# Two places in PSUM for half sums m1; columns of weights and means in one bank; first means in the images' places; another order in the beginning

## The chip, the cores and the metric

The kernel runs on one core of one Trainium2 chip. The metric is the device time of one execution in microseconds (us). The engines are named as in the profile: PE (matrix multiplication; PEld is its loading of weights), DVE (vector), ACT (scalar), POOL (general) and SP (which issues most transfers). Each engine takes its instructions in the order in which the program wrote them; an instruction that has to wait holds up all that stands behind it on its engine.

## What is computed

The input x has 160 images of 128 channels with 32x32 pixels. Each image is normalised over groups of four channels, then convolved (3x3, 128 to 128 channels, padding 1) with a weight set that is first quantised in two steps; there are five weight sets, each for 32 of the images. The result is added to x.

```python
beta, alpha = jnp.max(U), jnp.min(U)
s1 = (beta - alpha) / 3.0
v1 = s1 * floor(U / s1)
s2 = s1 / 5.0
v2 = s2 * floor((U - v1) / s2)
w = (v1 + v2).reshape(OUT_CH * N, IN_CH, K, K)          # N = 5 sets
act = conv_general_dilated(xb, w, strides (1, 1), padding 1, feature_group_count=N)
...
g = v.reshape(B_, 32, C_ // 32, H_, W_)                 # _gn: groups of 4 channels
m, s = mean(g, axis=(2, 3, 4)), var(g, axis=(2, 3, 4))
normalised = (g - m) / sqrt(s + eps)
x = x + conv(_gn(x), U)
```

## The kernel before

**One image.** The channels lie on the 128 partitions. The normalised image is kept as two float16 parts, a high one and a low one, which are convolved one after the other into the same sums. The 3x3 window is done as three columns of taps, in the order `COLS` = 1, 0, 2. Rows are taken in pairs: an even and an odd row of the output share products with sums and differences of rows of the input. The products with sums of rows are gathered in PSUM tile `m1`, those with differences in tile `m2` (16 half rows x 32, one bank each). An image's own sums stand in a pair of banks, `eo`; two such pairs take turns.

There are two kinds of images from image 7 on: even ones ("parted") take six matmuls for the half sums, 18 direct ones with the high part (line 629) and 12 short ones (line 668); odd ones ("combined") work on sums of rows for both parts and take 12 matmuls for half sums and 24 for the rest, all of line 668. Images 0 to 2 (`FIRST` = 3) are convolved without half sums; image 2 stands in the banks of m1 and m2 meanwhile.

**The order of one step.** `conv(i)` writes for PE: the half sums of the next image, `sums_of_pairs(i + 1)` (line 668: differences into m2, then sums into m1), and then the rest of image i, `rest_of_column`, on top of what `pairs(i)` has put into `eo`. After that ACT copies m2 of image i+1 to SBUF (`leave`, line 725) and DVE writes m1 + m2 and m1 - m2 into the next `eo` (`pairs`, lines 735 and 737). So in one step of the loop PE's sums for image i+1 must not overwrite m1 before DVE's line 737 has read it for image i, and PE's first matmul of the rest of image i needs line 737 as well. Between the two stand three matmuls of sums (parted) or six (combined).

Around this ACT measures later images (lines 194 and 201, sum and square), normalises (523, 531, 576) and takes finished images out of PSUM at half size (`residual`, line 754); POOL adds them to x by a transfer (773) and does the small arithmetic of the statistics (221 to 246) and two outer rows of a combined image (554, 555); DVE makes the low parts (589, 582) and the sums of rows (603 to 606, 565 to 571), measures some images itself (184 to 188) and quantises the next weight set in small portions (101 to 127, 463).

**Statistics of a group of images.** `means` is a matmul (line 210) into a small PSUM tile `pg`; ACT copies it (219, `ngm`); POOL makes deviations `dv` (221 to 224); `variances` is a second matmul (227) into `pg`; ACT reads it (233, `ve`), POOL makes `rstd` and `shift` (237 to 246), which `normalise` needs. **Columns of weights.** `turn_column` transposes three taps into PSUM tile `pt` (line 472); ACT writes them as `wt` (485) and, halved, as `half` (486); POOL makes four more from `half` (487 to 490). `pg` and `pt` have a bank each, m1 and m2 one each, `eo` four: all eight banks.

**The beginning.** Nothing is scheduled by a planner: the order on each engine is the order of the calls in `run`. For the first three images the calls are: the range of all weights (DVE), statistics 0 and 1, the three columns of set 0, direct products of images 0 to 2 column by column, and then the first three rounds of the loop, in which `residual` 2, 0 and 1, `measure(0, 11)` (image 11 is measured on DVE), `leave(3)`, `pairs(3)`, `low_part(4)` and `combinations(4)` stand. `sums_of_pairs(3)` is written in round 2.

Of the kernel before, what the change touches and what calls it, by code (L numbers as in the profile page):

```python
# [19 lines left out]
ROW = 3  # L20
# [139 lines left out]
class Statistics:  # L160
# [2 lines left out]

    size = 1024

    def __init__(self, nc, small, psum, gavg, mhalf, nb, scale, name):
        self.nc, self.small, self.psum, self.gavg, self.mhalf = nc, small, psum, gavg, mhalf
        self.nb, self.scale, self.name = nb, scale, name

        self.mv = self.tile("mv", [nb, 2])  # L170
# [32 lines left out]
            accum_out=self.mv[:, j, 1:2],  # L203
        )

    def means(self):
        self.pg = self.psum.tile(
            [self.nc.NUM_PARTITIONS, 2, self.nb], F32, tag="pg", name=f"pg{self.name}"
        )
        self.nc.tensor.matmul(  # L210
            self.pg[:, 0, :], self.gavg, self.mv[:, :, 0], start=True, stop=True
        )
# [36 lines left out]
def general_path(tc, keep, steps, x, u, out):  # L249
# [8 lines left out]
    with tc.If(far > 0), ExitStack() as ctx:  # L258
        one = ctx.enter_context(tc.tile_pool(name="g_one", bufs=1))
        psum = ctx.enter_context(tc.tile_pool(name="g_psum", bufs=1, space=PSUM))  # L260
        ident = one.tile([P, P], F32, tag="ident", name="g_ident")
        make_identity(nc, ident)
        gavg = group_mean_matrix(nc, one)
        mhalf = one.tile([P, 1], F32, tag="mhalf", name="g_mhalf")
        nc.gpsimd.memset(mhalf, -0.5)
        pad = one.tile([P, H + 2, W + 2], F32, tag="pad", name="g_pad")
        nc.gpsimd.memset(pad, 0.0)
        for n in range(N_SETS):
            un = one.tile([P, C, TAPS], F32, tag="u", name=f"g_u{n}")
            nc.sync.dma_start(un, uv[n])  # L270
            wn = one.tile([P, C, TAPS], F32, tag="w", name=f"g_w{n}")
            k1, k2 = run(steps.quantise(one, un, f"g{n}", F32))
            nc.vector.tensor_scalar_mul(wn, k1, steps.s1)
            nc.vector.scalar_tensor_tensor(wn, k2, steps.s2, wn, ALU.mult, ALU.add)
            wt = one.tile([P, TAPS, C], F32, tag="wt", name=f"g_wt{n}")
            for k in range(TAPS):
                pt = psum.tile([P, C], F32, tag="pt", name=f"g_pt{n}_{k}")
                nc.tensor.transpose(pt, wn[:, :, k], ident)
                nc.scalar.copy(wt[:, k, :], pt)
            with tc.For_i(0, IMGS // N_SETS, 1) as b:  # L280
                xt = one.tile([P, H * W], F32, tag="xt", name=f"g_xt{n}")
                nc.sync.dma_start(xt, xv[n, :, bass.ds(b, 1), :])
                stats = Statistics(nc, one, psum, gavg, mhalf, 1, 1.0, f"g{n}")
                stats.image(0, xt)
                stats.means()
# [24 lines left out]


class Main:
# [36 lines left out]
    def __init__(self, tc, ctx, keep, x, u, out):  # L349
# [9 lines left out]
        def pool(name, bufs, **kw):  # L359
# [15 lines left out]
        self.small = pool("small", 3)  # L375
        self.ps_eo = pool("ps_eo", 2, space=PSUM)
        ps_m = pool("ps_m", 1, space=PSUM)
        self.ps_stat = pool("ps_stat", 1, space=PSUM)
        self.ps_tr = pool("ps_tr", 1, space=PSUM)
        self.steps = Steps(nc, keep)  # L380

        self.pair = [
            ps_m.tile([P, self.H // 2, self.W], F32, tag=name, name=name) for name in ("m1", "m2")
        ]
        self.chunks, self.z, self.hi, self.v, self.eo, self.m2 = {}, {}, {}, {}, {}, {}
        self.sum = {}
        self.wts = {}
# [49 lines left out]
    def over_partitions(self, ext1, ident, between):  # L437


        nc, P = self.nc, self.P  # L440
        rows = self.ps_tr.tile([1, 2, P], F32, tag="pt", name="rows")
# [5 lines left out]
        spread = self.ps_tr.tile([P, 2], F32, tag="pt", name="spread")  # L447
        nc.tensor.matmul(spread, self.ones, top, start=True, stop=True)
        return spread

    def make_column(self, n, col, by_scalar=False):
# [5 lines left out]
        k1, k2 = yield from self.steps.quantise(self.qpool, un, f"{n}_{col}", MM, by_scalar)  # L457
        if n == 0:
            parts = ((k1, self.ident5), (k2, self.ident))
            self.keep_column(n, col, self.turn_column(n, col, parts))  # L460
# [5 lines left out]

    def turn_column(self, n, col, parts):
        nc, P = self.nc, self.P
        pt = self.ps_tr.tile([P, ROW, P], F32, tag="pt", name=f"pt{n}_{col}")
# [6 lines left out]
        return pt  # L476

    def keep_column(self, n, col, pt):


        nc, P = self.nc, self.P
        wt = self.wpool.tile([P, 6, P], MM, tag=f"wt{col}", name=f"wt{n}_{col}")
        half = self.qpool.tile([P, ROW, P], MM, tag="half", name=f"half{n}_{col}")
        outer = self.qpool.tile([P, P], MM, tag="outer", name=f"outer{n}_{col}")
        nc.scalar.mul(wt[:, self.G, :], pt, 2.0 / LIFT)  # L485
        nc.scalar.mul(half, pt, 1.0 / LIFT)
# [4 lines left out]
        self.wts[n, col] = wt  # L491


    def by_vector(self, i):
# [2 lines left out]
    def stats_of(self, k):  # L497
        if k not in self.stats:
            self.stats[k] = Statistics(
                self.nc, self.small, self.ps_stat, self.gavg, self.mhalf, len(self.groups[k]),  # L500
                self.steps.lift, k,
            )
        return self.stats[k]
# [160 lines left out]
    def product(self, target, i, kind, source, col, start, stop):  # L664
# [9 lines left out]
            skip_group_check=True,  # L674
        )

    def both(self, i):

        return [self.halves(v) for v in ([self.hi[i]] if self.combined(i) else []) + [self.v[i]]]

    def sums_of_pairs(self, i):

        both = self.both(i)
        for a, kind in ((1, self.DIFF), (0, self.SUM)):
            for col in self.COLS:
                for j, (_, st) in enumerate(both):
                    self.product(
                        self.pair[a], i, kind, st[:, a], col,
                        col == self.COLS[0] and j == 0,
                        col == self.COLS[-1] and j == len(both) - 1,  # L690
                    )
# [30 lines left out]
    def leave(self, i):  # L722

        m2 = self.evac.tile([self.P, self.H // 2, self.W], F32, tag="m2", name=f"m2_{i}")
        self.nc.scalar.copy(m2, self.pair[1])  # L725
        self.m2[i] = m2

    def pairs(self, i, between=lambda: None):


        nc = self.nc
        m1, m2 = self.pair[0], self.m2.pop(i)
        eo = self.eo[i] = self.bank_pair(i)
        rows = eo.rearrange("p h (i a) w -> p (h i) a w", a=2)
        nc.vector.tensor_add(rows[:, :, 0], m1, m2)  # L735
# [46 lines left out]
    def run(self):  # L782
# [44 lines left out]
        spread = self.over_partitions(ext1, ident, self.stats_of(0).means)  # L827

        def take(steps, count):
            for _ in range(count):  # L830
# [25 lines left out]
        self.stats[0].scales()  # L856
        take(second, 1)
        measure(1, 3)
        self.stats[1].means()
        self.stats[1].deviations()  # L860
        self.warm_up(14)
        parts(0)
# [3 lines left out]
        self.stats[1].scales()  # L866
        parts(1)
        run(first)
        self.warm_up(2)
        parts(2)  # L870
        take(second, 2)
# [11 lines left out]
        take(third, 1)  # L883
        measure(1, 4)
        run(second)
        measure(1, 5)
        parts(3)
        measure(0, 6, 7)
        measure(1, 6, 7)
        for i in range(self.FIRST):  # L890
# [11 lines left out]
        for i in range(self.imgs):  # L902
# [3 lines left out]
            def on_the_way(col):  # L906
                if col == self.COLS[1]:
                    for st in ready:
                        st.means()
                    for *column, parts in self.columns:  # L910
                        turned.append((column, self.turn_column(*column, parts)))
                    self.columns.clear()
                if col == self.COLS[2]:
                    for st in middle:
# [29 lines left out]
            if i < self.FIRST:  # L944
# [5 lines left out]
                if i == 2:  # L950
# [44 lines left out]
            if i < self.FIRST:  # L995
                for st in ready:
                    st.deviations()
            for column, pt in turned:
                self.keep_column(*column, pt)
            turned = []  # L1000

            if i >= self.FIRST:
# [70 lines left out]
```

## Time and profile before

| | |
|---|---|
| median of 4 runs | 992.46 us (991.67 to 993.86) |
| the profiled execution | 992.15 us, of which its span is 990.3 us |
| PE busy | 958.2 us, 97% |
| DVE busy | 927.7 us, 94% |
| ACT busy | 894.6 us, 90% |
| POOL busy | 386.3 us, 39% |
| bytes moved | 246.05 MB, mean 248 GB/s |

The span is the time from the first to the last instruction; 1.8 us of the execution lie around it. PE's clock was granted in full nearly throughout (mean 0.999). In the 40 slices of the page PE is busy 2 tenths in the first, 8 in the second, 9 or more in all others but the last (7). The views used below are the page, the waits (who waited for whom, in total), the chain of waits (followed back from the last instruction), the timeline of an engine (start, length, line, operation, output<-input), and the windows (busy time by stretch). One thing is needed to read PE's lines: matmuls overlap, and their ends are modelled. A matmul of 512 columns is given 379 ns, but the next one starts 216 ns after it when nothing holds it up.

### The profile page before, as it was taken

The numbers are of one execution on the slowest core, as the hardware profiler recorded it, in microseconds if no ns is written. First come the engines' busy times: TensorE is split into PE (matmuls) and PEld (weight loads), VectorE is DVE, ScalarE is ACT, GpSimd is POOL, SyncE is SP. The second block draws the span as 40 slices with busy tenths as digits, with TensorE's granted clock in tenths as the row PEclk, the third lists the DMA queues.
The fourth block names the chain that finished last, engine by engine and source line by source line (L and its number), as shares of the span: only waits on it lengthen the run. The fifth ranks groups of instructions, "written<-read, shape, count | busy, mean of one in ns | idle before, by whom it ended". The sixth has DMA issues, their size and how long they took to land.

```text
span 990.3 us, 16124 instructions
## 1 busy us (share of the span) xinstructions
PE 958.2 (97%) x5938; PEld 578.4 (58%) x5938; DVE 927.7 (94%) x1256; ACT 894.6 (90%) x1224; POOL 386.3 (39%) x565
## 2 busy tenths in 40 slices
PE   2899999999999999999999999999999999999997
PEld 1445655566656666666655666666665666666564
DVE  7999999999999999989999999999999998889995
ACT  5879999999999999999999999999999999998651
POOL 4324563633316253714343433315343424132410
PEclk9999999999999999999999999999999999999999
DMA  9538999999997989799898999998999898987764
GB/s 361 207 107 237 243 252 274 256 264 273 256 310 176 297 238 304 190 301 266 261 252 253 267 278 238 281 284 222 241 277 305 214 301 217 291 227 206 181 177 153
DMA packets 65129, 246.05 MB, mean 248 GB/s; under 512 B 5008, under 2 KB 5008, under 8 KB 65040
## 3 DMA queue, kind: packets, MB, share of 16 engines
q1 hardware_dynamic: 45312, 173.09, 50.0%
q0 software_dynamic: 19728, 71.84, 37.7%
q8 instruction: 48, 0.79, 0.3%
q14 instruction: 41, 0.34, 0.1%
HBM read 89.19 MB, written 83.89 MB: 175 GB/s over the span
## 4 chain that ended last, share of the span: by engine, by line
PE 72%; DVE 12%; ACT 7%; issue 3%; POOL 3%; DMA 2%; SPq 0%; DVEq 0%; ACTq 0%; POOLq 0%
PE eo L668 24%; PE m L668 24%; PE eo L629 23%; ACT junk L201 2%; ACT vh L576 2%; DVE eo L737 1%; DVE eo L735 1%; ACT sum L754 1%; DMA xt<-in_x_dram 1%; DVE lo L589 1%; DVE v L565 1%; POOL v L554 1%; POOL rstd L237 1%; DVE vl L582 1%; ACT m L725 1%
## 5 line engine op out<-in xcount | busy, mean ns | idle before, releaser
L668 PEld LDWEIGHTS <-wt 128*128 128x128 f16 x4266 | 417.2, 98 | 234.9 <-issue 6.5
L629 PE MATMUL eo<-hi,wt 128*128 128x496 f16 (+3 forms) x1422 | 339.6, 375 | 1.4 <-ACT wt L485 0.9
L773 POOL DMA_DIRECT2D xt<-sum x137 | 122.4, 899 | 463.8 <-ACT sum L754 449.6
L629 PEld LDWEIGHTS <-wt 128*128 128x128 f16 x1494 | 146.0, 99 | 141.9 <-ACT wt L485 2.3
L582 DVE SCALAR_TENSOR_TENSOR vl<-v,rstd,vh 128x2048 f16<-128x2048 f32 x80 | 188.1, 2351 | 4.3 <-ACT vh L576 4.3
L668 PE MATMUL eo<-vh,wt 128*128 128x248 f16 (+1 forms) x960 | 183.9, 273 | 0.0
L668 PE MATMUL eo<-vl,wt 128*128 128x248 f16 (+1 forms) x960 | 183.9, 273 | 0.0
L668 PE MATMUL m<-vh,wt 128*128 128x496 f16 (+1 forms) x480 | 182.2, 380 | 1.8 <-DVE eo L737 1.1
L668 PE MATMUL m<-vl,wt 128*128 128x496 f16 (+1 forms) x480 | 182.2, 380 | 0.2 <-DVE vl L582 0.2
L194 ACT ACTIVATE junk<-xt 128x1024 f16<-128x1024 f32 x152 | 160.6, 1057 | 17.5 <-DMA xt<-in_x_dram 13.9
L201 ACT ACTIVATE junk<-xt,mv 128x1024 f16<-128x1024 f32 x152 | 173.8, 1144 | 0.1
L576 ACT ACTIVATE vh<-v,rstd 128x2048 f16<-128x2048 f32 x80 | 160.8, 2011 | 2.5 <-POOL v L555 2.0
L754 ACT ACTIVATE sum<-eo 128x1024 f32<-128x1024 f32 x137 | 138.0, 1008 | 14.9 <-PE eo L668 14.8
L735 DVE TENSOR_TENSOR eo<-m,m 128x512 f32<-128x512 f32 x157 | 109.2, 695 | 36.3 <-ACT m L725 28.4
L668 PE MATMUL eo<-rows,wt 128*128 128x256 f16 (+1 forms) x924 | 138.9, 273 | 0.0
L668 PE MATMUL m<-rows,wt 128*128 128x496 f16 (+1 forms) x462 | 113.6, 380 | 0.5 <-DVE eo L737 0.2
L737 DVE TENSOR_TENSOR eo<-m,m 128x512 f32<-128x512 f32 x157 | 109.5, 697 | 3.6
L725 ACT COPY m<-m 128x512 f32<-128x512 f32 x157 | 90.5, 577 | 18.4 <-PE m L668 18.4
L523 ACT ACTIVATE z<-xt,shift,rstd 128x1024 f32<-128x1024 f32 x80 | 99.8, 1248 | 2.7 <-POOL shift L244 2.6
L589 DVE TENSOR_TENSOR lo<-z,hi 128x1024 f16<-128x1024 f32 x80 | 97.9, 1224 | 0.0
L565 DVE TENSOR_TENSOR v<-xt 128x960 f32<-128x960 f32 x80 | 92.0, 1149 | 0.0
L531 ACT CAST hi<-z 128x1024 f16<-128x1024 f32 x80 | 83.6, 1045 | 2.5
(111 smaller groups left out, 890.5 us busy)
## 6 DMA issues: line engine op xcount, KB each, us to landing
xt<-in_x_dram SPq DMA_DIRECT2D x78, 1024.0 KB, 9.5
out_dram<-xt SPq DMA_DIRECT2D x78, 1024.0 KB, 6.0
xt<-sum POOLq DMA_DIRECT2D x137, 512.0 KB, 6.2
u<-in_L_conv_U_dram SPq DMA_DIRECT2D x4, 576.0 KB, 9.0
xt<-in_x_dram SPq DMA_DIRECT2D x4, 512.0 KB, 9.5
range<-in_L_conv_U_dram SPq DMA_DIRECT2D x3, 576.0 KB, 7.6
out_dram<-xt SPq DMA_DIRECT2D x3, 512.0 KB, 2.8
u<-in_L_conv_U_dram SPq DMA_DIRECT2D x2, 288.0 KB, 2.9
```

Of the source, the lines that this page charges most:

```text
L194: self.nc.scalar.activation(junk, image, ACTF.Copy, scale=-1.0 / image.shape[1], accum_out=self.mv[:, j, 0:1],)
L201: self.nc.scalar.activation(junk, image, ACTF.Square, bias=self.mv[:, j, 0:1], accum_out=self.mv[:, j, 1:2],)
L565: nc.vector.tensor_sub(v[:, W:last], x[:, : last - W], x[:, 2 * W :])
L576: self.nc.scalar.mul(vh, self.v[i], st.rstd[:, j])
L582: self.nc.vector.scalar_tensor_tensor(vl, self.v[i], st.rstd[:, j], self.hi[i], ALU.mult, ALU.subtract)
L589: self.nc.vector.tensor_sub(lo[:, 1 : self.H + 1, :].rearrange("p h w -> p (h w)"), self.z.pop(i), self.hi[i].rearrange("p h w -> p (h w)"),)
L629: nc.tensor.matmul(self.bank(target, h)[:, r0 - h0 : r1 - h0, c0:c1], self.wts[n, col][:, k, :], tile[:, s0 : s0 + r1 - r0, c0 + dw : c1 + ...
L668: self.nc.tensor.matmul(target[:, :, c0:c1], self.wts[n, col][:, kind, :], source[:, :, c0 + dw : c1 + dw], start=start, stop=stop, skip_g ...
L735: nc.vector.tensor_add(rows[:, :, 0], m1, m2)
L737: nc.vector.tensor_sub(rows[:, :, 1], m1, m2)
L754: nc.scalar.mul(self.sum[i], eo.rearrange("p h r w -> p (h r w)"), 0.5)
L773: self.nc.gpsimd.dma_start(self.image(i), self.sum.pop(i), accum_op=ALU.add)
```

## The change

- m1 gets two places, `m1a` for images with even number and `m1b` for odd ones, in banks of their own; m2 stays one. Image 2 stands in m1a and m2.
- Eight banks being all there are, `pt` (384 columns) and `pg` (the other 128) become parts of one tile `small` in one bank. The first two groups' means lie in a pair of banks of `eo` that is not yet in use, and so do the rows for the weight range.
- `keep_column` is cut in three: `keep_taps` (wt), `keep_halves` (half) and `keep_sums` (POOL's four). For column 2 of set 0 the calls are now taps, means of group 2, halves, deviations of group 2, sums.
- `measure(0, 11)` moves from the end of round 1 to round 2, between `pairs(3)` and `low_part(4)`.

In the written order of the instructions PE, ACT and SP keep theirs. On POOL the four instructions of `keep_sums` of that column move behind the four of `deviations`. On DVE the five instructions of image 11's measurement move behind the two of `pairs(3)`. The number of instructions is the same on every engine. Of the waits, the one of the first sum into m1 for line 737 is gone in each step, and the loading of weights for the first matmul of `rest_of_column` waits for line 737 in its place. The matmul of group 2's means now waits for ACT's `wt` of column 2, and ACT's `half` waits for that matmul. At a later set's columns the transposing matmul waits for ACT's last reading of the shared bank.

```diff
-        self.ps_stat = pool("ps_stat", 1, space=PSUM)
-        self.ps_tr = pool("ps_tr", 1, space=PSUM)
+        ps_small = pool("ps_small", 1, space=PSUM)
...
-        self.pair = [
-            ps_m.tile([P, self.H // 2, self.W], F32, tag=name, name=name) for name in ("m1", "m2")
-        ]
+        self.m1a, self.m1b, self.m2_ps = (
+            ps_m.tile([P, self.H // 2, self.W], F32, tag=name, name=name)
+            for name in ("m1a", "m1b", "m2")
+        )
+        self.pair = [self.m1a, self.m2_ps]
+
+        small = ps_small.tile([P, 512], F32, tag="small", name="small")
+        self.pt, self.pg = small[:, : ROW * P].rearrange("p (k o) -> p k o", k=ROW), small[:, ROW * P :]
...
+    def m1(self, i):
+        return self.m1b if i % 2 else self.m1a
...
                     self.product(
-                        self.pair[a], i, kind, st[:, a], col,
+                        self.m2_ps if a else self.m1(i), i, kind, st[:, a], col,
...
-        m1, m2 = self.pair[0], self.m2.pop(i)
+        m1, m2 = self.m1(i), self.m2.pop(i)
...
-        self.stats[2].means()
+
+        self.keep_taps(0, self.COLS[2])
+        self.stats[2].means(self.pg)
+        half = self.keep_halves(0, self.COLS[2])
         self.stats[2].deviations()
+        self.keep_sums(0, self.COLS[2], half)
...
                     self.high_part(5)
                     self.pairs(3)
+                    measure(0, 11)
                     self.low_part(4)
                     run(self.combinations(4))
                 self.residual(j)
-                if i == 1:
-                    measure(0, 11)
```

More of the change, by code (lines that the diff above doesn't have):

```diff
@@ L164, with __init__ @@
     size = 1024
-    def __init__(self, nc, small, psum, gavg, mhalf, nb, scale, name):
-        self.nc, self.small, self.psum, self.gavg, self.mhalf = nc, small, psum, gavg, mhalf
+    def __init__(self, nc, small, gavg, mhalf, nb, scale, name):
+        self.nc, self.small, self.gavg, self.mhalf = nc, small, gavg, mhalf
         self.nb, self.scale, self.name = nb, scale, name
@@ L204, in image_square, with means @@
         )
[L206 to L209, printed above, removed]
+    def means(self, place):
+        self.pg = place[:, : 2 * self.nb].rearrange("p (k j) -> p k j", k=2)
         self.nc.tensor.matmul(
@@ L282, in general_path @@
                 nc.sync.dma_start(xt, xv[n, :, bass.ds(b, 1), :])
-                stats = Statistics(nc, one, psum, gavg, mhalf, 1, 1.0, f"g{n}")
+                stats = Statistics(nc, one, gavg, mhalf, 1, 1.0, f"g{n}")
                 stats.image(0, xt)
-                stats.means()
+                stats.means(psum.tile([P, 2], F32, tag="pg", name=f"g_pg{n}"))
                 stats.deviations()
@@ L440, in over_partitions @@
         nc, P = self.nc, self.P
-        rows = self.ps_tr.tile([1, 2, P], F32, tag="pt", name="rows")
+        place = self.bank_pair("range").rearrange("p h r w -> p h (r w)")
+        rows = place[0:1, 0, : 2 * P].rearrange("p (k c) -> p k c", k=2)
         for k in range(2):
@@ L446, in over_partitions @@
         nc.vector.tensor_reduce(top, rows, AX.X, ALU.max)
-        spread = self.ps_tr.tile([P, 2], F32, tag="pt", name="spread")
+        spread = place[:, 1, :2]
         nc.tensor.matmul(spread, self.ones, top, start=True, stop=True)
@@ L459, in make_column @@
             parts = ((k1, self.ident5), (k2, self.ident))
-            self.keep_column(n, col, self.turn_column(n, col, parts))
+            self.turn_column(n, col, parts)
         else:
@@ L468, in turn_column @@
         nc, P = self.nc, self.P
-        pt = self.ps_tr.tile([P, ROW, P], F32, tag="pt", name=f"pt{n}_{col}")
+        pt = self.pt
         for k in range(ROW):
@@ L475, in turn_column, with keep_taps, keep_halves, keep_sums @@
                 )
-        return pt
-    def keep_column(self, n, col, pt):
-        nc, P = self.nc, self.P
+    def keep_taps(self, n, col):
+        P = self.P
         wt = self.wpool.tile([P, 6, P], MM, tag=f"wt{col}", name=f"wt{n}_{col}")
-        half = self.qpool.tile([P, ROW, P], MM, tag="half", name=f"half{n}_{col}")
+        self.nc.scalar.mul(wt[:, self.G, :], self.pt, 2.0 / LIFT)
+        self.wts[n, col] = wt
+    def keep_halves(self, n, col):
+        half = self.qpool.tile([self.P, ROW, self.P], MM, tag="half", name=f"half{n}_{col}")
+        self.nc.scalar.mul(half, self.pt, 1.0 / LIFT)
+        return half
+    def keep_sums(self, n, col, half):
+        nc, P, wt = self.nc, self.P, self.wts[n, col]
         outer = self.qpool.tile([P, P], MM, tag="outer", name=f"outer{n}_{col}")
-        nc.scalar.mul(wt[:, self.G, :], pt, 2.0 / LIFT)
-        nc.scalar.mul(half, pt, 1.0 / LIFT)
         nc.gpsimd.tensor_tensor(outer, half[:, 0, :], half[:, 2, :], ALU.add)
@@ L490, in keep_column @@
         nc.gpsimd.tensor_scalar_mul(wt[:, self.MINUS_G2, :], wt[:, 2, :], -1.0)
-        self.wts[n, col] = wt
+    def keep_column(self, n, col):
+        self.keep_taps(n, col)
+        self.keep_sums(n, col, self.keep_halves(n, col))
     def by_vector(self, i):
@@ L499, in stats_of @@
             self.stats[k] = Statistics(
-                self.nc, self.small, self.ps_stat, self.gavg, self.mhalf, len(self.groups[k]),
+                self.nc, self.small, self.gavg, self.mhalf, len(self.groups[k]),
                 self.steps.lift, k,
@@ L724, in leave @@
         m2 = self.evac.tile([self.P, self.H // 2, self.W], F32, tag="m2", name=f"m2_{i}")
-        self.nc.scalar.copy(m2, self.pair[1])
+        self.nc.scalar.copy(m2, self.m2_ps)
         self.m2[i] = m2
@@ L826, in run @@
             self.measure(i)
-        spread = self.over_partitions(ext1, ident, self.stats_of(0).means)
+        first_means = self.bank_pair("means").rearrange("p h r w -> p h (r w)")
+        spread = self.over_partitions(
+            ext1, ident, lambda: self.stats_of(0).means(first_means[:, 0])
+        )
         def take(steps, count):
@@ L858, in run @@
         measure(1, 3)
-        self.stats[1].means()
+        self.stats[1].means(first_means[:, 1])
         self.stats[1].deviations()
@@ L868, in run @@
         run(first)
+        self.keep_column(0, self.COLS[0])
         self.warm_up(2)
@@ L885, in run @@
         run(second)
+        self.keep_column(0, self.COLS[1])
         measure(1, 5)
@@ L908, in on_the_way @@
                     for st in ready:
-                        st.means()
+                        st.means(self.pg)
                     for *column, parts in self.columns:
-                        turned.append((column, self.turn_column(*column, parts)))
+                        self.turn_column(*column, parts)
+                        turned.append(column)
                     self.columns.clear()
@@ L997, in run @@
                     st.deviations()
-            for column, pt in turned:
-                self.keep_column(*column, pt)
+            for column in turned:
+                self.keep_column(*column)
             turned = []
```

## The prediction

> **What bounds the kernel now.** I read the page first, then PE's waits, then the chain of waits, and last the timeline of single steps.
>
> ```profile
> PE 958.2 (97%) x5938; PEld 578.4 (58%) x5938; DVE 927.7 (94%) x1256; ACT 894.6 (90%) x1224; POOL 386.3 (39%) x565
> ...
> PE 72%; DVE 12%; ACT 7%; issue 3%; POOL 3%; DMA 2%; SPq 0%; DVEq 0%; ACTq 0%; POOLq 0%
> ...
> L668 PE MATMUL m<-vh,wt 128*128 128x496 f16 (+1 forms) x480 | 182.2, 380 | 1.8 <-DVE eo L737 1.1
> ```
>
> PE has 32 us of idle time in 990.3. Of these 17.0 are the first wait for the weight range and 6.4 lie in the last 10.3 us (the window 980 to 990.3 has PE busy for 3.86). The wait that the change aims at, m1 for line 737, shows as 1.3 us. That is too little, since the modelled ends cover a part: a parted image's six matmuls of half sums take 1.46 us when nothing holds them, and a start follows the last by 0.216. The loss is read from the starts:
>
> ```profile
> 188.64 0.38 PE L668 MATMUL m<-vl,wt 128*128 128x496 f16 x1
> 189.57 0.38 PE L668 MATMUL m<-vh,wt 128*128 128x512 f16 x1 [0.55 <-DVE eo L737]
> ...
> 478.96 0.81 PE L668 MATMUL m<-rows,wt 128*128 128x512 f16 x3
> 479.97 0.81 PE L668 MATMUL m<-rows,wt 128*128 128x512 f16 x3 [0.20 <-DVE eo L737]
> ```
>
> 189.57 - 188.64 - 0.216 = 0.71 us lost, where the view says 0.55; in the second place, 479.97 - 478.96 - 3 x 0.216 = 0.36. Read in this way, m1's wait costs, in us by the time where it stands: 0.31 (66.8), 0.70 (152.9), 0.71 (189.6), 0.27 (196.9), 0.03 (201.5), 0.27 (225.9), 0.20 (338.7), 0.11 (385.8), 0.36 (480.0), 0.18 (527.2), 0.19 (715.2), 0.05 (762.2), 0.27 (918.8) and 0.05 (952.6): 3.7 us. That is the most that a second m1 can give by itself. The chain tells which of it counts:
>
> ```profile
> 101.13 0.13 PE pg L210 x2
> 101.29 0.16 ACT ngm L219
> ...
> 114.61 5.45 POOL v L554
> ...
> 187.04 0.48 ACT m L725
> 187.55 0.70 DVE eo L735
> ...
> 196.15 0.71 DVE eo L737
> ...
> 196.91 0.81 PE m L668 x3
> ```
>
> From 101 to 197 us the chain has no matmul: ACT, POOL and DVE set the pace, and PE only waits for them at times. ACT runs without a gap of more than 0.13 us from 181.8 to beyond 225, and its copy of m2 for image 28 (ends 211.24) lets DVE's line 735 start (211.27); so I take this stretch as lasting to DVE's line 582 and 737 at 224.5 and 225.85. After that the chain is PE to 393.5, a detour over ACT, POOL and transfers to 479.9, PE to 902, DVE to 918.8, PE.
>
> **The beginning, step by step.**
>
> ```profile
> 49.03 0.06 ACT ngm L219
> ...
> 50.92 0.18 POOL dv L221
> ...
> 52.01 0.38 PE pg L227 x2
> 52.40 2.58 PE eo L629 x12
> ...
> 55.00 1.22 DVE xt L765
> 56.23 1.21 DVE st L184 x2
> ...
> 57.91 0.62 DVE eo L735
> 58.55 0.70 DVE eo L737
> 59.25 1.14 DVE lo L589
> ```
>
> *Weights, means, POOL's order.* The means' matmul (47.83 now) has to wait for ACT's wt, which ends at 48.65. It then starts at 48.70, and the direct products behind it, which start at 48.70 now, begin 0.25 later (the same pair of matmuls takes 0.25 at 52.01). ACT's half waits for it (end 48.70 + 0.37), so half runs 49.13 to 49.61 and ngm ends near 49.65, 0.57 later than now; behind them ACT has 3.36 us of idle time before ve, which hides that. POOL's four dv instructions (1.08 from 50.88 to 51.96) then run 49.70 to 50.78 instead of behind the four of the weights (49.11 to 50.88). PE's two blocks of direct products take 2 x 1.28 from 48.95: 51.51. The variances no longer wait: 51.51 in place of 52.01, a gain of 0.50. POOL's four for the weights go 50.78 to 52.6; their first reader is PE's difference for column 2 near 54.7, and rstd starts behind them at 52.62, not 52.69. So ACT's z (54.45), hi and the copy of m2 for image 3 (56.67 to 57.25) move by 0.07 only. The cover there is thin: the four instructions cost 1.8 at 49.11 but 3.65 for the first column (29.85 to 33.50). If they cost that here, rstd and all of the beginning come up to 1.83 later; unlike 29.85, DVE is at its statistics as at 49.11, so I take 1.8.
>
> [...]
>
> *Image 11's measurement behind pairs(3).* DVE now goes without a gap from 55.00 to 66.79. Afterwards residual 0 runs 54.50 to 55.7, and pairs(3) waits for ACT's copy, 57.18: 57.24 to 58.64 (59.25 now). PE's first matmul of image 3 moves from 59.31 to 58.70, a gain of 0.61. But DVE has stood idle for 1.5 us that the measurement filled before, and its 1.7 us now stand ahead of low_part(4): 60.25 in place of 59.16, and all that follows is 1.09 late. Queued behind it: rows of image 4 (ready 62.86; PE wants them at 62.26 and has them at 62.92, against 62.87 now, +0.05), rows of image 5 (66.53; PE's differences start at 66.59 instead of 65.88, +0.71), pairs(4) (67.87). Here the second m1 helps: the sums don't wait (0.31 of that is saved), and the first matmul of image 4 starts at 67.93 against 67.48: **+0.45**. The means of group 3 need image 11: ready 60.27, wanted 60.41, hidden by 0.14. After 68 us I find no PE wait with less than 0.8 us of slack up to 101 that the second m1 doesn't widen (the one at 73.39 gets 0.65, three sums), and ACT's ngm at 83.78 and 101.29 wait for PE: the 0.45 go into the stretch that isn't PE's.
>
> **The stretch of ACT, POOL and DVE, 101 to 226.** The waits of 0.70, 0.71, 0.27 and 0.03 us go, since the rest of an image wants line 737 only 0.65 or 1.30 us later; but PE then runs into the next thing that these engines deliver. That is line 582 at 224.51 + 0.45; from there PE goes through five differences and six sums without the 0.27 us of m1's wait: 0.45 - 0.27 = **+0.18** behind image 31.
>
> **The rest.** PE sets the end here and every lost m1 wait counts: 0.20 + 0.11 + 0.36 + 0.18 + 0.19 + 0.05 = 1.09, and 0.27 + 0.05 = 0.32 in the end: **-1.41**. Each is below what the moved wait leaves (0.65 with three sums, 1.30 with six). The wait on weight loading ahead of the rest costs nothing where it is met; as a bound, 157 such waits at 0 to 5 ns (line 668's first difference with two waits starts 0.110 after a 248-column matmul, as the others do) give 0 to 0.8. The later sets' transposing matmuls wait for readings that ended over 0.7 us before: nothing. No transfer is added or moved; SP's order is the same.
>
> **Sum:** 0.18 - 1.41 = -1.2 us on 992.15: 990.9. The profiled execution is 0.3 below the median of the runs, 992.46, which would give 991.2; I say 991.1. From all bounds (start 0.5 better or 1.83 worse than worked out, weight loading 0 to 0.8) this case goes from 989.6 to 993.0. What can be told from no change is about 0.2%, 2 us.
>
> **Rivals.**
> *All waits come back.* If ACT and DVE between 101 and 226 follow PE after all, the whole 3.7 counts, and with the beginning better by 0.5 it is 4.2; half way between that and the forecast is -2.7: 989.5 (988.0 to 990.3). For it: DVE's pairs wait for ACT's copy of m2 and this for PE's differences, in 34 places (28.4 us). Against it: ACT's row without gaps.
>
> [...]
>
> *A blocked POOL instruction, the slower side.* Line 554 takes 0.29 us at 54.58 and 5.45 at 114.61, where ACT stands idle for 1.46 us until it ends; line 237 takes 1.04 at 52.69 and 5.10 at 402.93, both on the chain. POOL and DVE are shifted against each other by 0.5 to 1.1 us, so such a block can fall elsewhere. One more on the chain costs 5.1 less ACT's usual cover of 1.4: -1.2 + 3.7 = +2.5: 994.7. It decides from a block of about 2.6 us on (1.4 cover and 1.2 gain).
>
> *It doesn't do what it says:* line 737 is waited for again, only later, and the gain is nil while the beginning's 0.45 stay: 992.6. Against it: all lost waits are shorter than the sums that stand between.
>
> **Chances.** Forecast 0.44 (0.03 of it under -0.2%, 0.01 over +0.2%), all waits back 0.34 (0.01 of it within 0.2%), blocked POOL 0.17 (0.02 within), nil 0.05. Faster by over 0.2%: 0.03 + 0.33 = 0.36; within: 0.40 + 0.01 + 0.02 + 0.05 = 0.48; slower: 0.16. The range takes in the forecast's own and most of the first rival's, and stops short of the POOL case: 988.6 to 993.8.
>
> **What will show it.** Right: no PE wait of line 668 for 737; the variances of group 2 near 51.5; DVE idle for 1.5 us ahead of pairs(3), and PE's first matmul of image 4 near 67.9; PE's rest of image 31 at 227.4 (227.2 now). Wrong: the last at 226 or earlier (first rival), ACT idle next to a POOL instruction of over 3 us at a new place (second), or waits of line 629 or 668 for 737 at the same times as now (third).

## The result, and the profile after

| | before | changed |
|---|---|---|
| median, runs side by side | 991.68 us (52 runs, 991.30 to 993.86) | 990.70 us (32 runs, 989.96 to 991.57) |
| ratio | | 0.9987, 95% interval 0.9982 to 0.9991 |
| the profiled execution | 992.15 us, span 990.3 | 992.0 us, span 990.3 |
| PE / DVE / ACT / POOL busy | 958.2 / 927.7 / 894.6 / 386.3 us | 958.7 / 928.0 / 895.0 / 405.3 us |

The ratio is a gain of 1.3 us (0.9 to 1.8). The profiled execution of the changed kernel lies above the median of its runs; why is shown below. The page of that profile (in its first line the busy time of each engine, in its second the shares of the chain, in its third a group of instructions with its idle time):

```profile
PE 958.7 (97%) x5938; PEld 578.6 (58%) x5938; DVE 928.0 (94%) x1256; ACT 895.0 (90%) x1224; POOL 405.3 (41%) x565
...
PE 80%; ACT 7%; DVE 6%; issue 3%; POOL 2%; DMA 0%; SPq 0%; DVEq 0%; ACTq 0%; POOLq 0%
...
L682 PE MATMUL m<-vh,wt 128*128 128x496 f16 (+1 forms) x240 | 91.1, 380 | 1.0 <-ACT m L742 1.0
```

The line that stood before as `m<-vh` x480 is now cut in three, m (m2), m1a and m1b, and its idle time before is no longer DVE's 737 (now 754), but ACT's copy of m2 (742). Lines have moved: 668 is 682, 629 is 643, 735 and 737 are 752 and 754, 725 is 742, 589 and 606 are 603 and 620, 582 is 596, 554 and 555 are 568 and 569, 565 is 579, 576 is 590, 523 is 537, 463 is 468, 472 is 477, 765 is 782, 210 is 209, 227 is 226, 485 and 486 are 486 and 491. PE's waits of the same profile (total us, how often, longest):

```profile
PE m L682 <- DVE rows L620: 1.1, 3, 0.5
PE m L682 <- ACT m L742: 1.0, 1, 1.0
...
PE eo L643 <- DVE eo L754: 0.5, 1, 0.5
...
PE m L682 <- DVE vl L596: 0.2, 1, 0.2
```

No half sum waits for line 754 any more; the one wait for it left is that of image 3's direct products. The places shown before at 188.64 and 478.96 look like this now, on PE's timeline:

```profile
188.87 0.38 PE L682 MATMUL m<-vh,wt 128*128 128x512 f16 x1 [1.00 <-ACT m L742]
...
189.95 0.38 PE L682 MATMUL m<-vl,wt 128*128 128x496 f16 x1
190.17 0.38 PE L682 MATMUL m1b<-vh,wt 128*128 128x512 f16 x1
...
479.71 0.81 PE L682 MATMUL m<-rows,wt 128*128 128x512 f16 x3
480.36 0.81 PE L682 MATMUL m1a<-rows,wt 128*128 128x512 f16 x3
```

From the last difference to the first sum it is 190.17 - 189.95 = 0.22 us (0.93 before), and from the first of three differences to the first sum 0.65 (1.01 before). Both gaps are closed. But ahead of the first there is a new one of 1.00 us for ACT's copy of m2.

To compare two profiles, I use the **shift**: the start of one PE instruction in the one less the start of the same instruction in the profile of before. It was read in every profile at the same places: at PE's transposing matmul at 38.79 us, at the first sum into m1 for image 5 (66.83), at 187.8, at 226.5 and at the last matmul (983.59). At 38.79 it differs from -0.08 to +0.46 without any tie to the kernel (0.14 and 0.00 for one and the same), so this is taken off the other four:

| profile of | 38.8 (taken off) | 66.8 | 187.8 | 226.5 | end |
|---|---|---|---|---|---|
| changed kernel, first profile (clock dip) | 0.20 | +1.08 | +1.11 | +0.85 | -0.53 |
| changed kernel again | 0.22 | +0.39 | +0.41 | +0.15 | -1.22 |
| one_m1 | 0.07 | +1.08 | +1.10 | +1.11 | +0.59 |
| before_m11 | -0.03 | +1.15 | +1.18 | +1.19 | +0.66 |
| whole_column | 0.08 | +0.48 | -0.19 | -0.44 | -1.82 |
| m11_back (clock dip) | 0.14 | -0.25 | -1.02 | -1.27 | -2.65 |
| m11_back again | 0.00 | -0.92 | -0.95 | -1.21 | -2.60 |
| m11_whole | 0.20 | -0.30 | -0.36 | -0.63 | -2.01 |
| pad_early | 0.20 | +0.39 | +1.13 | +0.08 | -1.30 |
| pad_late | 0.01 | +0.41 | -0.35 | -0.61 | -0.05 |
| edge25 (clock dip) | -0.08 | +1.06 | +0.42 | +0.16 | -1.22 |
| m11_edges | 0.46 | -0.91 | -0.94 | -1.20 | -2.58 |

(The other kernels are those of the experiments below.) The prediction in these terms was +0.45 just behind 66.8 (at the first matmul of image 4), +0.18 at 226.5 and -1.23 at the end. The rows are taken up one by one.

### The profile page after: what moved, and what is told of

Same layout as the page of the kernel before. It is cut to its first block, busy times and chain, and to the rows that moved or that the text cites. A ratio compares the mean times of both kernels' runs of the same rounds, so it can differ in the third digit from the quotient of the medians.

```text
span 990.3 us, 16122 instructions
## 1 busy us (share of the span) xinstructions
PE 958.7 (97%) x5938; PEld 578.6 (58%) x5938; DVE 928.0 (94%) x1256; ACT 895.0 (90%) x1224; POOL 405.3 (41%) x565
## 4 chain that ended last, share of the span: by engine, by line
PE 80%; ACT 7%; DVE 6%; issue 3%; POOL 2%; DMA 0%; SPq 0%; DVEq 0%; ACTq 0%; POOLq 0%
PE eo L682 27%; PE eo L643 26%; PE m L682 13%; PE m1b L682 9%; PE m1a L682 5%; ACT junk L201 2%; ACT vh L590 2%; POOL v L568 1%; ACT sum L771 1%; ACT z L537 1%; ACT m L742 1%; DVE lo L603 1%; DVE ext L432 1%; DVE ext L433 1%; DMA range<-in_L_conv_U_dram 0%
## 5 line engine op out<-in xcount | busy, mean ns | idle before, releaser
L596 DVE SCALAR_TENSOR_TENSOR vl<-v,rstd,vh 128x2048 f16<-128x2048 f32 x80 | 188.2, 2352 | 3.6 <-ACT vh L590 3.6
L682 PE MATMUL m<-vh,wt 128*128 128x496 f16 (+1 forms) x240 | 91.1, 380 | 1.0 <-ACT m L742 1.0
L682 PE MATMUL m<-vl,wt 128*128 128x496 f16 (+1 forms) x240 | 91.1, 380 | 0.2 <-DVE vl L596 0.2
L682 PE MATMUL m1b<-vh,wt 128*128 128x496 f16 (+1 forms) x225 | 85.4, 380 | 0.0
L682 PE MATMUL m1b<-vl,wt 128*128 128x496 f16 (+1 forms) x225 | 85.4, 380 | 0.0
L752 DVE TENSOR_TENSOR eo<-m1a,m 128x512 f32<-128x512 f32 x78 | 54.3, 697 | 30.7 <-ACT m L742 28.2
```

The lines of the kernel that those rows point to most:

```text
L596: self.nc.vector.scalar_tensor_tensor(vl, self.v[i], st.rstd[:, j], self.hi[i], ALU.mult, ALU.subtract)
L682: self.nc.tensor.matmul(target[:, :, c0:c1], self.wts[n, col][:, kind, :], source[:, :, c0 + dw : c1 + dw], start=start, stop=stop, skip_g ...
```

## The experiments

**1. The changed kernel once more.** No edit; the first profile had an oddity between 39 and 47 us that had to be told from the change.

> The changed kernel once more, for a second profile and as the partner of the three others. Theory (a late start of +0.45 us from image 11's measurement, handed on by ACT, POOL and DVE to 226 us, then -0.27 there and -1.41 to the end): 1.2 us below the kernel before, ratio 0.9988. In the profile, PE's first matmul of image 4 (line 643) lies 0.45 us behind that of before once a clock dip like the one at 41 to 45 us of the first profile is absent, and the rest of image 31 0.2 us behind; at the end PE is 1.2 us ahead.

Measured: 990.9 us, ratio 0.9990 (0.9981 to 0.9999), span 989.5. The oddity is gone. In the first profile PE's clock was granted at half. The windows (busy time of PE, PEld, DVE, ACT, POOL, each with its number of instructions, then the granted clock) show it; first the changed kernel, then the one before:

```profile
41.00:43.00 2.00, 2.00 (x7) 0.68 (x6) 1.83 (x4) 1.97 (x4) 1.92 (x4) 0.50 0.03 8
```

```profile
41.00:43.00 2.00, 2.00 (x11) 0.89 (x10) 1.82 (x4) 1.97 (x4) 1.94 (x3) 1.00 0.00 0
```

PE is "busy" for all of the 2 us in both, but with 7 matmuls in place of 11. By the shift, with 0.20 taken off, it came up to 1.7 us late (1.88 at 41.7); the waits behind it at 48.7 and 52.0 took up a part, and 1.08 - 0.39 = 0.69 us stayed. Without the dip the beginning goes as predicted. The chain of the second profile (start, length, what):

```profile
48.50 0.38 ACT wt L486
...
48.92 0.40 PE small L209 x2
...
49.41 0.49 ACT half L491
49.90 0.06 ACT ngm L218
...
50.91 0.20 POOL dv L223
51.11 0.38 POOL outer L498
...
54.59 1.25 ACT z L537
...
56.81 0.59 ACT m L742
57.43 0.71 DVE eo L752
58.16 0.70 DVE eo L754
58.86 1.20 DVE st L184 x2
...
60.54 1.14 DVE lo L603
```

Against the chain before, the means come ahead of `half`, POOL's `dv` ahead of `outer`, `pairs` (752, 754) ahead of the measurement (184). DVE's timeline shows the price, idle time ahead of the pairs:

```profile
54.60 1.23 DVE L782 SCALAR_TENSOR_TENSOR xt<-eo,xt 128x1024 f32<-128x1024 f32 x1 [0.36 <-PE eo L643]
57.43 0.70 DVE L752 TENSOR_TENSOR eo<-m1b,m 128x512 f32<-128x512 f32 x1 [1.60 <-ACT m L742]
```

**2. The measurement of image 11 put back** (m11_back, taken twice):

```diff
                     self.pairs(3)
-                    measure(0, 11)
                     self.low_part(4)
                     run(self.combinations(4))
                 self.residual(j)
+                if i == 1:
+                    measure(0, 11)
```

> The changed kernel with image 11's measurement back at the end of round 1, ahead of pairs(3). Theory: DVE has no idle time of 1.5 us ahead of pairs(3); PE's first matmul of image 4 comes 0.8 us earlier than before (1.25 earlier than with the change), this is handed on through ACT's stretch, and the time is 2.5 us below the kernel before: ratio 0.9975, that is 1.3 us below the changed kernel. Rival A (the beginning is worth nothing either way, the gain is m1 alone): as the changed kernel, 0.9987. Rival B (the moved measurement brings PE forward, which is what helps): 0.6 us above the changed kernel, 0.9993.

Measured: 989.57 us, ratio 0.9975 (0.9965 to 0.9985). This is faster than the changed kernel by about 1.2 us: the highest of its runs, 990.14, lies below all but one of the eleven runs of the changed kernel that stood beside it (990.02 to 992.36). Its profile had the clock dip, so there is a second one.

> The same kernel as m11_back, once more, for a second time and for a profile in which PE's clock does not dip at 40 to 45 us (the first one's did, and PE was up to 1.8 us late there). Theory: without a dip the variances of group 2 stand near 51.5 + the offset of the weight range, the first matmul of image 4 is 0.5 us earlier than in m11_whole, ratio to the kernel before 0.9975 to 0.9980. Rival (POOL's order is worth nothing): as m11_whole, 0.9984, and the gap between the two profiles is only the POOL instruction at 176 us.

Measured: 989.52 us, ratio 0.9978 (0.9969 to 0.9987). DVE now uses the time in which it stood idle for the measurement, and the pairs are 0.23 us earlier, not later:

```profile
54.37 1.22 DVE L782 SCALAR_TENSOR_TENSOR xt<-eo,xt 128x1024 f32<-128x1024 f32 x1 [0.34 <-PE eo L643]
55.51 1.28 DVE L184 BATCH_NORM_STATS2 st<-xt 128x6 f32<-128x512 f32 x2
...
57.20 0.70 DVE L752 TENSOR_TENSOR eo<-m1b,m 128x512 f32<-128x512 f32 x1
```

(0.22 of the 0.23 is the shift at 38.8, so the pairs stand where they stood in the changed kernel, and the measurement came for nothing.) At 66.8 the two profiles differ by 0.39 + 0.92 = 1.31 us, and by 1.38 at the end.

**3. One place for m1**, and **4. the kernel before with the measurement alone moved**:

```diff
     def m1(self, i):
-        return self.m1b if i % 2 else self.m1a
+        return self.m1a
```

```diff
                     self.pairs(3)
+                    measure(0, 11)
...
-                if i == 1:
-                    measure(0, 11)
```

> The changed kernel with all sums in m1a, so that each first sum waits for line 754 again (m1b stays as an unused bank). Theory: the wait at image 5 is back (0.65 us), so the start is 1.1 us behind the kernel before, and the later waits of 1.4 us are back too: 1.1 us above the kernel before, ratio 1.0011. Rival A: as the kernel before, 1.0000. Rival B: 0.6 us below it, 0.9994.

> The kernel before with the one edit that image 11's measurement stands behind pairs(3). Theory: DVE is 1.1 to 1.2 us later from low_part(4) on, nothing takes that up before 226 us: 1.2 us above the kernel before, ratio 1.0012. Rival A: 1.0000. Rival B: PE's image 3 0.5 us earlier and kept, 0.9994.

Measured: one_m1 993.1 us, ratio 1.0013 (1.0004 to 1.0022); before_m11 992.85 us, 1.0012 (1.0003 to 1.0021). So by the times the moved measurement costs 1.2 us on either kernel, and the second place for m1 is worth 1.0013 - 0.9990 = 0.0023, 2.3 us. Each ratio is uncertain by 0.0009, and the ends of the profiles in the table say 2.60 - 1.22 = 1.38 us for the move on the changed kernel, 0.66 on the kernel before, and 0.59 + 1.22 = 1.81 for the second place. What that is made of in the beginning is seen at image 5's half sums, in PE's timeline of one_m1 and of the changed kernel (second profile):

```profile
66.65 0.82 PE L682 MATMUL m<-rows,wt 128*128 128x512 f16 x3 [0.48 <-DVE rows L620]
67.99 0.81 PE L682 MATMUL m1a<-rows,wt 128*128 128x512 f16 x3 [0.52 <-DVE eo L754]
```

```profile
66.78 0.82 PE L682 MATMUL m<-rows,wt 128*128 128x512 f16 x3 [0.48 <-DVE rows L620]
67.44 0.81 PE L682 MATMUL m1b<-rows,wt 128*128 128x512 f16 x3
```

With one place the sum starts 1.34 us behind the first difference, with two 0.66. In the table both kernels keep their +1.1 up to 226.5 and lose 0.5 behind it: where PE comes later, the waits that it met at 385.8 (0.11) and 480.0 (0.36) are over before it gets there: the shift steps down by 0.12 and 0.36 at these two places.

**5. POOL's order undone**, on the changed kernel (whole_column) and on m11_back (m11_whole):

```diff
-        self.keep_taps(0, self.COLS[2])
+        self.keep_column(0, self.COLS[2])
         self.stats[2].means(self.pg)
-        half = self.keep_halves(0, self.COLS[2])
         self.stats[2].deviations()
-        self.keep_sums(0, self.COLS[2], half)
```

> The changed kernel with one part undone: the third column is kept whole (both of ACT's copies and POOL's four instructions) before the means of group 2, as the kernel before had it. Theory: the earlier variances (about 52.0 in place of 51.5) are worth nothing while image 11 is measured behind the pairs of image 3, because these pairs then wait for ACT's copy of m2 at 57.2, and DVE stands idle ahead of them anyway. PE's first matmul of image 3 and all behind it stay where they are in the changed kernel, within 0.1 us. Ratio to the kernel before 0.9988 to 0.9991. Rival: the 0.5 us counts by itself: 0.9993 to 0.9996. Second rival, that the order on POOL costs: below 0.9985.

> The same undone on top of m11_back (image 11 measured at the end of round 1, third column kept whole before the means). Here the pairs of image 3 stand behind the measurement of image 11 and this behind residual 0, which waits for PE's direct products, so theory says the 0.5 us of the variances goes through to the first matmul of image 3: 0.4 to 0.5 us later than m11_back in a profile without a dip of PE's clock at 40 to 45 us, ratio to the kernel before 0.9980 (m11_back had 0.9975). Rival: POOL's order is worth nothing here either: 0.9975.

Measured: 990.44 us, 0.9991 (0.9982 to 1.0000), and 990.18 us, 0.9984 (0.9975 to 0.9993). The times cannot part these by themselves; the table can. On the changed kernel the order is worth 0.48 - 0.39 = 0.09 us at 66.8, on m11_back 0.92 - 0.30 = 0.62. The earlier variances only help where DVE has work to do in the time won: with the measurement moved away, pairs(3) waits for ACT's copy either way.

**6. Nine matmuls added, early and late.** They take PE's time, and their result is overwritten by the half sums behind them. In pad_early they stand ahead of image 24, as here, in pad_late ahead of image 104:

```diff
         both = self.both(i)
+        if i == 24:
+            for _ in range(9):
+                self.product(self.m1(i), i, self.SUM, both[0][1][:, 1], 1, True, True)
```

> The changed kernel with nine matmuls added ahead of the half sums of image 24 (at 183 us, 9 x 0.216 = 1.94 us of PE's time; their result is overwritten by the half sums). Theory: from 101 to 226 us ACT, POOL and DVE set the pace, so PE takes this up in its waits at 188.2 (1.05 lost there), 196.2 (0.21) and 222.9 (0.70): step of +1.94 at 183, near 0.9 behind 188.2, 0.7 behind 196.2, at most 0.1 behind 226. Ratio to the kernel before 0.9988 to 0.9992, as the changed kernel. Rival, that PE sets the pace here as elsewhere (and that the removed waits of 0.70 and 0.71 should have counted): +1.94 up to the end, less 0.3 at 916.8: 1.0006.

> The same nine matmuls ahead of the half sums of image 104, where the theory has PE setting the end: +1.94 stays up to 916.8, where a wait for DVE takes up 0.33 at most: +1.6 at the end, ratio to the kernel before 1.0005 to 1.0008, 0.0016 above pad_early. Rival, that slack is spread over the whole kernel alike: as pad_early.

Measured: 990.72 us, 0.9990 (0.9981 to 0.9999), as the changed kernel; and 992.66 us, 1.0010 (1.0001 to 1.0019). The same 1.94 us cost nothing at 183 us, and 992.66 - 990.72 = 1.94 at 654 (equal to the hundredth by luck, as each ratio is uncertain by 0.0009, but no run of the one reaches the times of the other). The table agrees: at 226.5 pad_early stands at +0.08, where the changed kernel stands at +0.15, and from there to the end pad_late goes from -0.61 to -0.05, 0.56 up, where the others go 1.37 to 1.39 down. Here my expectation missed: up to 0.33 of the 1.94 us was to be taken up in the wait for DVE's low parts at 916.8, which is as long in pad_late as in the changed kernel (0.16 in both views). PE's timeline of pad_early:

```profile
182.87 2.11 PE L682 MATMUL m1a<-rows,wt 128*128 128x512 f16 x9
184.81 0.81 PE L682 MATMUL m<-rows,wt 128*128 128x512 f16 x3
...
188.90 0.38 PE L682 MATMUL m<-vh,wt 128*128 128x512 f16 x1
...
222.85 0.35 PE L477 MATMUL small<-ident,m 128*128 128x128 f16 x3 [0.34 <-DVE m L468]
```

The half sums of image 24 start 1.87 us later than in the second profile of the changed kernel (182.94), the differences of image 25 by 0.71 (188.19 there) and without a wait, and the transposing matmuls by -0.09 (222.94 there). From 183 to 226 us PE isn't what counts. For 101 to 183 us no work was added; there the chain of the kernel before says it. The two largest waits for m1 stood in this stretch (0.70 and 0.71): they were removed, and came back as waits for ACT's copy (1.00 at 188.2), DVE's rows (0.16 at 196.2) and DVE's weights, line 468 (0.65 at 222.9).

**7. The blocked POOL instruction.** Undoing POOL's order had moved the end by 0.6 us in a place that it doesn't touch: whole_column's shift falls from +0.48 to -0.19 by 187.8. The cause stands on POOL's timeline at 177 us, first of the changed kernel (second profile), then of whole_column:

```profile
176.82 5.32 POOL L568 TENSOR_SCALAR v<-xt,ngm 128x32 f32<-128x32 f32 x1
182.13 0.28 POOL L569 TENSOR_SCALAR v<-xt,ngm 128x32 f32<-128x32 f32 x1
```

```profile
176.70 1.32 POOL L568 TENSOR_SCALAR v<-xt,ngm 128x32 f32<-128x32 f32 x1
177.95 1.30 POOL L569 TENSOR_SCALAR v<-xt,ngm 128x32 f32<-128x32 f32 x1
```

and on DVE's, in the same order:

```profile
176.78 1.15 DVE L579 TENSOR_TENSOR v<-xt 128x960 f32<-128x960 f32 x1
...
181.65 0.42 DVE L620 TENSOR_TENSOR rows<-lo 128x512 f16<-128x512 f16 x1
```

```profile
176.75 1.14 DVE L579 TENSOR_TENSOR v<-xt 128x960 f32<-128x960 f32 x1
```

POOL's instruction took 5.3 us where it started 0.04 to 0.05 us behind DVE's line 579 (before, both profiles of the changed kernel, one_m1, before_m11, m11_back again, m11_whole, pad_early), and 1.3 where it started 0.05 ahead (whole_column, m11_back's first, pad_late). In the second profile of the changed kernel the long one ends at 182.14, 0.07 us behind the end of DVE's last subtraction of rows (182.07): it lasted through eight of DVE's instructions, the first of 1.15 us, and ended 0.16 us after the start of the ninth, line 752 (181.98). I call such an instruction blocked; that DVE holds it up is inferred from these times, and by what was not shown. To price it, the two rows of image 25 went to DVE on the changed kernel (edge25), and those of images 15 and 25 on m11_back (m11_edges):

```diff
+        engine = nc.vector if i in (25,) else nc.gpsimd
-        nc.gpsimd.tensor_scalar(v[:, :W], x[:, W : 2 * W], minus, -1.0, ALU.add, ALU.mult)
-        nc.gpsimd.tensor_scalar(
+        engine.tensor_scalar(v[:, :W], x[:, W : 2 * W], minus, -1.0, ALU.add, ALU.mult)
+        engine.tensor_scalar(
             v[:, last : H * W], x[:, last - W : last], minus, 1.0, ALU.add, ALU.mult
```

> The changed kernel with the two edge rows of image 25 (128x32 each) formed by DVE in place of POOL. In the profiles so far POOL's first of these took 5.3 us where it started 0.04 to 0.05 us after DVE's 128x960 subtraction (before, after, after_again, m11_whole, pad_early, one_m1) and 1.3 us where it started 0.05 us before it (whole_column, m11_back, pad_late). Theory: this decides 0.70 us on ACT and at the end of the stretch; without the POOL instruction ACT's vh of image 25 starts 0.5 earlier, PE's step at 187.6 is about -0.16 in place of +0.54, and the end is 0.7 us earlier than in after_again: ratio to the kernel before 0.9980 to 0.9987. Rival: the block is hidden, the 0.7 us come from elsewhere: 0.9990 and a step of +0.54.

> m11_back with the edge rows of images 15 and 25 formed by DVE. At 115 us POOL's instruction took 5.45 us in every profile, and ACT stood idle for 1.45 us until it ended. Theory: ACT sets this stretch, so it gains up to 1.45 there, of which a part is lost again where ACT then waits for PE's means (0.15 us of slack at 161.8, and what PE itself gains at 134): 0.7 to 1.4 us less than m11_back: ratio to the kernel before 0.9961 to 0.9970. Rival, that POOL's block is covered: as m11_back, 0.9975 to 0.9980.

Measured: edge25 990.74 us, 0.9990 (0.9981 to 0.9999): not faster than the changed kernel. In its profile the step comes as expected (from +1.06 at 66.8 to +0.42 at 187.8, 0.64 us), but that profile had the clock dip, which took 0.67 at the start. That the block costs about 0.7 us in a profile is shown: whole_column, the first of m11_back, pad_late and edge25, which don't have it, fall by 0.64 to 0.77 from 66.8 to 187.8 (the second profile of the changed kernel goes from +0.39 to +0.41), and of the two profiles of the changed kernel and edge25 with the dip, the one without the block ends 1.22 - 0.53 = 0.69 earlier. What it costs in the median of the runs stays open. The changed kernel's own runs lie in two groups, 11 of 32 from 989.96 to 990.33 and the others from 990.57 on, and edge25's lowest, 990.05, isn't below the first, so some of its runs may go without the block as they are. And six of edge25's eleven runs have a granted clock of 0.996 or 0.997, which among the profiles only the three with the dip have. m11_edges 989.56 us, 0.9980 (0.9971 to 0.9989): no gain over m11_back. ACT's timeline has the reason, first m11_back's second profile, then m11_edges:

```profile
119.43 2.00 ACT L590 ACTIVATE vh<-v,rstd 128x2048 f16<-128x2048 f32 x1 [1.46 <-POOL v L569]
```

```profile
118.34 2.01 ACT L591 ACTIVATE vh<-v,rstd 128x2048 f16<-128x2048 f32 x1
...
144.71 2.00 ACT L591 ACTIVATE vh<-v,rstd 128x2048 f16<-128x2048 f32 x1 [1.91 <-POOL v L570]
```

The wait at 119 is gone, and one of 1.91 us stands at 144.7. POOL's timeline, in the same order, shows its instruction for image 19:

```profile
139.31 1.14 POOL L568 TENSOR_SCALAR v<-xt,ngm 128x32 f32<-128x32 f32 x1
```

```profile
138.88 5.54 POOL L569 TENSOR_SCALAR v<-xt,ngm 128x32 f32<-128x32 f32 x1
```

The block has moved to the next place. Of the 1.55 us that ACT had gained at 119 (119.43 - 118.34 and the 0.46 taken off above), 0.65 were gone before the new block, at 125, where ACT waits for PE. My expectation of 0.7 to 1.4 us was wrong, and its rival gave the right time for another reason than the one it named.

## Why the prediction was right

The time, 990.7 us, lies 0.4 below the forecast of 991.1, and the 1.3 us gained are near its sum of -1.2. That the time itself came so near has some luck in it: the forecast started from 992.15 to 992.46, and beside the changed kernel the kernel before took 991.68. By its steps, from the second profile with 0.22 taken off:

- **Weights, means, POOL's order.** Direct products 0.25 later at 48.70: measured 0.25. Variances at 51.51: 51.71 - 0.22 = 51.49.
- **Image 11's measurement.** First matmul of image 3 at 58.70: measured 58.70 (58.92 - 0.22). DVE idle for 1.5 us ahead of the pairs: 1.60. PE's differences for image 5 at 66.59: 66.56. In sum +0.45 predicted, +0.43 measured at the first matmul of image 4 (+0.39 at 66.8), the second m1's 0.31 among it.
- **The stretch from 101 to 226.** -0.27 predicted, 0.39 - 0.15 = 0.24 measured. The wait of 0.70 at 152.9 was given back, 0.15 at 175.4 and 0.54 at 187.6. ACT's timeline, before and in the second profile, shows who took it: ACT's z waits for POOL's shift, 0.57 longer.

```profile
175.27 1.24 ACT L523 ACTIVATE z<-xt,shift,rstd 128x1024 f32<-128x1024 f32 x1 [1.79 <-POOL shift L244]
```

```profile
175.90 1.24 ACT L537 ACTIVATE z<-xt,shift,rstd 128x1024 f32<-128x1024 f32 x1 [2.36 <-POOL shift L243]
```

At the end of the stretch PE met DVE's line 468 first (0.65 at 222.9) and line 596 only for 0.1 behind it; the prediction had named the latter alone (line 582, at 224.51). The rest of image 31 starts at 227.57 - 0.22 = 227.35; predicted 227.4.

- **The rest.** -1.41 predicted, 0.15 + 1.22 = 1.37 measured, and 1.37 to 1.39 in every other profile with two places that has no padding behind 226.

Of the rivals, *all waits come back* falls with pad_early and the step just shown: between 101 and 226 the two large waits of PE didn't count. *It doesn't do what it says* falls with the waits view and one_m1. *A blocked POOL instruction* was priced at 3.7 us, 5.1 less a cover of 1.4. That misreads the row at 114.6: the 1.46 us there are what ACT stood idle, so the cover was 5.45 - 1.46 = 4.0 and the price 1.46. Before 226 us no block of 5 us came at a new place (POOL's line 236 took 3.15 at 215.4, 2.01 before, and ACT had no gap beside it). Behind 226 new ones came (5.26 us at 356.0, 5.27 at 543.9, 5.39 at 778.7 in the second profile; POOL's busy time is 19 us higher on the page too) and cost nothing, since PE sets the pace there and the end is as predicted. The one that flips between profiles (image 25) is worth about 0.7 there; ACT had work for all but 0.51 us of it. That such an instruction can be long or short is shown (5.32 and 1.32 us), the price was five times too high.

The prediction was blind on two points. It put the first part of the beginning at a gain of 0.50 and 0.61 and the beginning as a whole at a loss of 0.45, but did not ask what the parts are worth without each other. Separately they are: the move +1.2 us by the times on either kernel (by the profiles +1.38 and +0.66), POOL's order -0.6 at 66.8 with the measurement at its old place and -0.1 behind the move, the second m1 -2.3 (by the profiles -1.8). The best of these leaves the move out. And it did not foresee that PE's clock drops to 0.50 at 40 us in 3 of 13 profiles.

In the second profile the means start behind `wt` (at 48.92, `wt` ends at 48.88). The second m1 is worth 1.8 to 2.3 us, of 3.7 of its waits.

## What to carry to other kernels

A wait in the profile is worth its length only where its engine sets the pace; to know it, add the same work early and late and see which of the two is paid for (here 0 and 1.94 us of 1.94). Work that another engine does while it would wait anyway costs nothing where it stands, even if a wait seems to come from it (here image 11's measurement, which cost 1.2 us where it was moved to): before moving it, look at what the engine will do in that time. And a gain of one part can be hidden by another part of the same change (POOL's order: 0.62 us at 66.8 without the move, 0.09 with it), so that each is best undone by itself.

## What had not been expected

**PE's clock.** In 3 of 13 profiles (first of the changed kernel, first of m11_back, edge25) the clock was granted at 0.50 around 40 to 43.5 us (in the first: 0.53 in the microsecond from 40, 0.50 in the next two, 0.76 in the fourth; in each of the three 1.71 us are missing to the full clock, which is 3.4 us at 0.50), in the ten others at 1.00 from 41 to 43 us. In the 11 profiles other than those of m11_back again and m11_edges PE does little from 37 to 39 us (0.13 to 0.96 us busy), and the three with the dip aren't those with the least (0.69 to 0.78). In the first profile PE's longest wait between 18 us and the dip is 1.30 us, for DVE's line 114, up to 38.99. What brings the dip, and what picks the profiles, was not shown. PE comes out of it 1.7 us late, and at 66.8 0.67 to 0.69 us of that are left.

**A race of 0.05 us.** Which of DVE and POOL starts first at 177 us shifts PE by about 0.7 us in the profile. At 115 us POOL's start is recorded 0.30 us ahead of DVE's and it is blocked all the same (5.44 or 5.45 us in each profile that has it), so the recorded start doesn't decide by itself. What does stays open.
